# Retention projections of blocks 3 to 7: seven float32 products of matrix halves, or three float32r products of 12-bit parts

## The chip, the core and the metric

The kernel runs on one core of a Trainium2 chip. The metric is the device time of one launch in microseconds (us). The kernel before takes 971.28 us, the median of three runs (969.27 to 971.3).

## The reference, cut to what matters

The input x has 4 sequences of 1024 tokens with 512 channels. Two layers stand in a sandwich of layer norms.

```python
x = x + _layernorm(_L0_attn_ref(_layernorm(x)))    # retention
x = x + _layernorm(_L0_ffn_ref(_layernorm(x)))     # gated FFN, inner width 1536
# retention, on the normed x:
q = x @ Wq.T ; v = x @ Wv.T                        # 512 x 512 each
ret = _retention_scan(v, lam)                      # state = lam * state + v_t, per channel
out = _layernorm(q * ret)
out = (out * silu(x @ Wg.T)) @ Wo.T
# FFN: weights rounded to fp8 values
fuse = silu((x @ gate_w) * gate_scale) * ((x @ up_w) * up_scale)
y = (fuse @ down_w) * down_scale
```

So every block of tokens has four square projections (v, q, g and o, 512 by 512) and the three FFN products.

## The kernel before

**Blocks and loops.** The 4096 tokens are cut into 8 blocks of 512. The outer loop t runs over the FFN of block t (`Ffn`, gate, up, down). Beside it the same pass does the retention of block t+1 (`b`, class `Retention`) and prepares block t+2 (`n`: load, first norm, transposition through DRAM into `xnT`). The inner loop i runs over 12 slices of 128 inner channels. In a slice TensorE does `gate(i)`, `up(i)` and `down(i-2)`, 8 matmuls of 128x128 by 512 each, and between these groups the projections of the next block. One slice takes 5.4 to 12.4 us.

**FFN number format.** The fp8-valued weights are exact in float32r (F32R in the code, a 4-byte format that TensorE reads in fewer bits), and the activations are cut into an upper and a lower part, so `project` does two float32r matmuls for each 128 channels.

**Projections in blocks 2 to 7 (`b.fast`).** v, q, g and o are each done with seven products of matrix halves in place of eight (`order`, `banks`, `product`, `take`, `add_o`), in plain float32. A product is four float32 matmuls of 256 columns. It needs sums of halves of the input (`input_sums`, on GpSimd, kept in `t_sums`), sums of halves of the weights (formed in block 0's and block 1's passes and kept in DRAM by `keep_sums`), and additions of the results, on VectorE, into `mids`. The weights' halves come through a ring of four 256 KB buffers (`w_ring`, `fetch_weights`): after each product the DMA for the fourth product ahead is put on SyncE's queue, where it waits until its buffer is free.

**What sets the order.** `keep_in_program_order` makes each engine execute its instructions in the order in which the program names them, so the order is written out by hand with `if t == ... and i == ...`. PSUM has eight banks: two for the projections (`pa0`, `pa1`), two that gate and up of the FFN use in turn (`pf`), four for down. A matmul group that begins in a bank waits until the engine that read the bank's previous content is done. So `up(i+1)` waits until VectorE has done the fused multiplication `fuse(i)` (SCALAR_TENSOR_TENSOR gate<-pfu), and a product in `pa1` waits until VectorE or ScalarE has read the product before it there.

**The end of a pass.** In i = 9 to 11 VectorE does, in this order: moments of x1, `fuse(9)`, the norm of x1 for token groups 0 and 1 with their transposition, `o_moments(2)` and `(3)`, `rest(9)`, `fuse(10)`, moments of x1 for groups 2 and 3, their norms, `fuse(11)`, `rest(10)` and the lower parts of the next FFN's input (`rest_of`). The next pass's `gate(0)` needs all of these. At the same time GpSimd does four `input_sums` for block n, and n's first three products run in i = 11.

**Block 1's pass (t = 1).** At the end of i = 0 `output_sums` forms the sums of the halves of Wo in place in `wo_sb`, on VectorE, and `keep_sums` stores them. ScalarE checks the FFN weights for values over the fp8 range in the same pass (`find_over`).

The lines most spoken of later:

```python
        pg = ps_f.tile([P, TB], F32, tag="pf", name=f"pfg_{self.t}_{i}")     # gate
        self.pu = ps_f.tile([P, TB], F32, tag="pf", name=f"pfu_{self.t}_{i}")  # up
        dve.scalar_tensor_tensor(g, self.pu, us_sb[:, i : i + 1], g, ALU.mult, ALU.mult)  # fuse
        act.copy(f[:, 0, :], g)
        dve.tensor_tensor(f[:, 1, :], self.g.pop(i), f[:, 0, :], ALU.subtract)            # rest
```

## Time and profile before

| what | value |
|---|---|
| median of 3 runs | 971.28 us |
| profiled execution, first to last instruction (span) | 968.2 us |
| the rest of a run, by the median | 3.1 us |
| TensorE (PE) busy | 955.3 us, 99% |
| VectorE (DVE) busy | 677.9 us, 70% |
| ScalarE (ACT) busy | 406.1 us, 42% |
| GpSimd (POOL) busy | 283.2 us, 29% |
| mean granted TensorE clock | 0.997 |
| DMA | 119.04 MB, mean 123 GB/s |

For the profiled execution the profile has no time but its span; the 3.1 us are the difference to the median of the runs. Times within the profile are counted from the first instruction. Engines are called by the profile's short names. "a <- b" means that a is written from b; names are those of the program's tiles, with f32 and fp32r for the two formats. A TensorE busy share says little about its rate, since matmuls overlap; the distance between starts of groups does.

### The profile page before, as it was taken

To read this page: it belongs to the slowest core of one execution; us is meant where nothing else is said; L and a number is where in the kernel's file an instruction comes from. 1 tells how busy PE (TensorE), PEld (TensorE's weight loads), DVE (VectorE), ACT (ScalarE), POOL (GpSimd) and SP (SyncE) were. 2 spreads that over 40 slices of the span, in tenths; PEclk is the share of its full clock that TensorE was granted. 3 is DMA by queue.
4 is the path that set the end of the run, shared out by engine and by line. 5 is a ranking of instruction groups with operands and counts; after the bars stand their busy time and mean duration, and the time that the engine had idled before them with its cause. 6 is when DMAs were issued, how large, how long until landed. Compare 5 with 4: busy or idle time off the path is not lost.

```text
span 968.2 us, 11802 instructions
## 1 busy us (share of the span) xinstructions
PE 955.3 (99%) x4118; PEld 764.9 (79%) x4118; DVE 677.9 (70%) x1038; ACT 406.1 (42%) x637; POOL 283.2 (29%) x356
## 2 busy tenths in 40 slices
PE   9999999999999999999999999999999999999997
PEld 7455767778888888888888888888888888888885
DVE  5996999676768578575685766867667675747445
ACT  3555674468656135331433315332153421524223
POOL 1405121402327042250522415242142512314020
PEclk9999999999999999999999999999999999999998
DMA  9311423762436336463236523364242632314021
GB/s 297 128 53 57 152 66 96 221 217 86 142 97 180 126 91 214 127 191 95 97 109 175 161 80 126 103 171 146 77 152 87 184 121 77 109 44 131 0 88 44
DMA packets 96060, 119.04 MB, mean 123 GB/s; under 512 B 8320, under 2 KB 58240, under 8 KB 96000
## 3 DMA queue, kind: packets, MB, share of 16 engines
q1 hardware_dynamic: 95136, 117.62, 39.6%
q8 instruction: 33, 0.54, 0.2%
q10 hardware_dynamic: 864, 0.66, 0.2%
q14 instruction: 27, 0.22, 0.1%
HBM read 86.00 MB, written 32.24 MB: 122 GB/s over the span
## 4 chain that ended last, share of the span: by engine, by line
PE 87%; DVE 6%; DMA 2%; ACT 2%; POOL 1%; issue 1%; SPq 0%; DVEq 0%; ACTq 0%; POOLq 0%
PE pfg L74 16%; PE pfu L74 16%; PE pd L74 15%; PE pq L74 10%; PE pv L74 10%; PE pg L74 9%; PE po L74 8%; DVE scr L74 1%; DVE st L74 1%; DVE y L74 1%; PE pt L74 1%; DMA xnT<-mx 1%; ACT x1n L74 1%; DVE gate L74 1%; POOL mv L74 1%
## 5 line engine op out<-in xcount | busy, mean ns | idle before, releaser
L74 PE MATMUL pfu<-x1nT,up_sb 128*128 128x512 f32 x768 | 205.1, 409 | 0.0
L74 PE MATMUL pfg<-x1nT,gate_sb 128*128 128x512 f32 x768 | 198.1, 400 | 0.1
L74 PE MATMUL pd<-down_sb,fuse 128*128 128x512 f32 x720 | 189.4, 405 | 0.0
L74 PEld LDWEIGHTS pfu<-x1nT,up_sb 128*128 128x128 f32 x768 | 144.5, 188 | 32.1 <-issue 3.1
L74 PEld LDWEIGHTS pfg<-x1nT,gate_sb 128*128 128x128 f32 x768 | 144.2, 188 | 30.3 <-DVE x1nT L74 0.9
L74 PEld LDWEIGHTS pd<-down_sb,fuse 128*128 128x128 f32 x720 | 135.4, 188 | 27.3
L74 ACT ACTIVATE gate<-pfg,gs_sb 128x512 f32<-128x512 f32 x96 | 65.5, 682 | 169.1 <-PE pfg L74 168.9
L74 ACT CAST fuse<-gate 128x512 fp32r<-128x512 f32 x90 | 55.6, 618 | 176.3 <-DVE gate L74 176.2
L74 DVE SCALAR_TENSOR_TENSOR gate<-pfu,us_sb,gate 128x512 f32<-128x512 f32 x96 | 71.8, 748 | 57.9 <-PE pfu L74 56.5
L74 POOL TENSOR_SCALAR mv<-mv 128x1 f32<-128x1 f32 (+1 forms) x82 | 23.5, 286 | 264.0 <-DVE mv L74 260.8
L74 DVE TENSOR_TENSOR fuse<-gate,fuse 128x512 fp32r<-128x512 f32 x90 | 76.8, 853 | 5.5 <-ACT fuse L74 5.5
L74 POOL TENSOR_TENSOR ysum<-y 128x256 f32<-128x256 f32 (+1 forms) x14 | 14.3, 1024 | 195.7 <-DVE y L74 195.7
L74 DVE BATCH_NORM_STATS2 st<-x 128x6 f32<-128x512 f32 x64 | 43.6, 681 | 29.4 <-POOL x L74 26.2
L74 POOL TENSOR_TENSOR mv<-mv,nhalf 128x1 f32<-128x1 f32 (+1 forms) x75 | 48.6, 649 | 6.2
L74 PE MATMUL pv<-t_sums,w_ring 128*128 128x256 f32 x192 | 45.5, 380 | 0.5 <-POOL t_sums L74 0.5
L74 PE MATMUL pg<-t_sums,w_ring 128*128 128x256 f32 x192 | 45.7, 381 | 0.0
L74 PE MATMUL po<-w_ring,t_sums 128*128 128x256 f32 x192 | 45.4, 379 | 0.0
L74 POOL TENSOR_TENSOR x<-x,x1n 128x512 f32<-128x512 f32 x32 | 41.5, 1296 | 13.2 <-ACT x1n L74 12.8
L74 PE MATMUL pq<-t_sums,w_ring 128*128 128x256 f32 x192 | 45.3, 379 | 0.0
L74 PEld LDWEIGHTS pv<-t_sums,w_ring 128*128 128x128 f32 x192 | 36.1, 190 | 6.6 <-POOL t_sums L74 0.7
L74 PEld LDWEIGHTS pg<-t_sums,w_ring 128*128 128x128 f32 x192 | 35.9, 190 | 6.5 <-ACT mids L74 1.3
L74 PEld LDWEIGHTS po<-w_ring,t_sums 128*128 128x128 f32 x192 | 36.2, 189 | 6.0 <-issue 0.3
(168 smaller groups left out, 1512.5 us busy)
## 6 DMA issues: line engine op xcount, KB each, us to landing
kept<-x SPq DMA_DIRECT2D x32, 256.0 KB, 3.0
x<-kept SPq DMA_DIRECT2D x32, 256.0 KB, 4.1
x<-in_x SPq DMA_DIRECT2D x28, 256.0 KB, 4.3
out<-d SPq DMA_DIRECT2D x27, 256.0 KB, 2.0
xnT<-mx SPq DMA_DIRECT2D x24, 256.0 KB, 4.9
w_ring<-dsum_v SPq DMA_DIRECT2D x24, 256.0 KB, 3.5
w_ring<-dsum_q SPq DMA_DIRECT2D x24, 256.0 KB, 2.6
w_ring<-dsum_g SPq DMA_DIRECT2D x24, 256.0 KB, 2.6
```

Of the source, the lines that this page charges most:

```text
L74: return lambda *args, **kwargs: tc.keep_in_program_order(op(*args, **kwargs))
```

## The change

Block 2 keeps its seven products per projection. In blocks 3 to 7, v, q and g are done with three float32r products instead; o stays as it was. A number is cut into its upper 12 bits (`top`) and the rest (`low`); `diff` holds a scaled difference of the two. Each of the four 128-channel output slices c of a projection gets three passes of four matmuls of 512 columns: top times top, low times low, then ScalarE multiplies the bank in place by 1 + 2**-12, and diff times diff completes the sum (`begin`, `end`, placed by the table `gaps`). After that v's slice is scanned, q's multiplied and g's given to Silu directly from the bank.

The parts of x are formed for each of the five blocks in i = 9 and 10 of the pass before (`tops_of`, `lows_of`, `diffs_of`), in quarters of 128x512 elements. The parts of the weights are formed once, in block 1's pass, 12 units of 128x512 (`Splitter`), stored to DRAM and fetched through a second ring in 36 pieces per block where 21 halves were fetched.

```diff
     def output_sums():
-        operands["o"] = {1: v[:, 0:2, 0:H], 2: v[:, 2:4, 0:H], 3: v[:, 2:4, H:D]}
+        operands["o"] = {}
+        made["o"] = {1: b11, 2: b21, 3: b22}
+        keep_sums("o")
         made["o"] = {5: b11, 7: b12, 6: b22, 4: b21}
         dve.tensor_tensor(b11, b12, b11, ALU.subtract)
...
+    class Splitter:
+            self.room = wpool.tile([P, 4, D], F32, tag="wo_sb", name="split_room")
...
+        def load(self, n):
+                src = self.sources[k].rearrange("(c p) f -> p c f", p=P)[:, :, ts(c, P)]
+                sp.dma_start(w.rearrange("p (c f) -> p c f", c=NC), src)
...
+                sp.dma_start(parts["top"].rearrange("p (c f) -> p c f", c=NC), src)
...
+        def split(self):
+                dve.tensor_scalar(top.bitcast(I32), w.bitcast(I32), TOP_MASK, None, ALU.bitwise_and)
+                dve.tensor_tensor(w, w, top, ALU.subtract)
+                dve.scalar_tensor_tensor(top, top, -LOW, w, ALU.mult, ALU.add)
+                pool.tensor_scalar(w, w, 1.0 / LOW, 1.0, ALU.mult, ALU.mult)
...
+        def store(self):
+                self.load(self.n + 1)
+                sp.dma_start(operands[k, c]["diff"], top)
+                sp.dma_start(operands[k, c]["low"], w)
...
+    gaps = {
+        -2: [("begin", "v", 0)], -1: [("end", "v", 0), ("begin", "v", 1)],
+        0: [("end", "v", 1)], 1: [("begin", "v", 2)], 2: [("end", "v", 2), ("begin", "v", 3)],
...
+        13: [("begin", "g", 1)], 14: [("end", "g", 1)], 15: [("begin", "g", 2)],
+        16: [("end", "g", 2)], 17: [("begin", "g", 3)], 18: [("end", "g", 3)],
...
+    def tops_of(self, *which):
+                dve.tensor_scalar(top, x, TOP_MASK, None, ALU.bitwise_and)
+    def lows_of(self, *which, engine=dve):
+                engine.tensor_tensor(self.quarter(self.low, k), x, top, ALU.subtract)
+    def diffs_of(self, *which):
+                dve.scalar_tensor_tensor(
+                    self.quarter(self.diff, k), low, -1.0 / LOW, top, ALU.mult, ALU.add
+                )
...
+    def begin(self, k, c, home):
+            bank = self.bank[k, c] = ps_tile(f"p{k}{c}_{self.t}", home)
+            self.pass_of(bank, k, c, "top")
+            self.pass_of(bank, k, c, "low")
+            act.activation(bank, bank, AF.Copy, scale=1.0 + LOW)
...
     def var(self):
-            var = ps_tile(f"var_{self.t}", "pa1" if self.fast else "pa")
+            var = ps_tile(f"var_{self.t}", "pa0" if self.by_parts else "pa1" if self.fast else "pa")
...
+            if t == 1 and 1 <= i < 9:
+                splitter.split()
...
+            if fast and i == 10 and n:
+                n.diffs_of(0, 1)
...
+            if t == 1 and i in (2, 3, 4, 7):
+                splitter.store()
+                splitter.split()
...
                 if n:
-                    n.input_sums(1, 2)
+                    n.new_parts()
+                    n.tops_of(0, 1, 2, 3)
+                    n.lows_of(0, 1, engine=pool)
+                    n.lows_of(2, 3)
...
                 b.x1_moments(2)
                 b.x1_moments(3)
+                if n:
+                    n.diffs_of(2, 3)
...
+            if t == 1 and 1 <= i < 9:
+                splitter.store()
```

Where these stand in the order: the first `split` of a slice comes after `gate(i)` and the projection work that follows it; the second, in i = 2, 3, 4 and 7, after `up(i)` and before `fuse(i)`, directly behind the load of its unit; `store` ends a slice. `tops_of` and `lows_of` come in i = 9 after the norms of x1's groups 0 and 1, `diffs_of(0, 1)` in i = 10 before `up(10)` and `fuse(10)`, `diffs_of(2, 3)` after x1's moments of groups 2 and 3 and before their norms. `gap(3i)`, `gap(3i+1)` and `gap(3i+2)` follow `gate(i)`, `up(i)` and `down(i-2)`; gap -2 and -1 lie in i = 11 of the pass before.

## The prediction

> **What bounds the kernel now.** I read the page first, then the chain, then the timelines of PE and DVE at the end of a pass, last the stretch of block 1's pass that gets the weight split.

> The page and its chain of waits:

> ```profile
> PE 955.3 (99%) x4118; PEld 764.9 (79%) x4118; DVE 677.9 (70%) x1038; ACT 406.1 (42%) x637; POOL 283.2 (29%) x356
> ...
> PE 87%; DVE 6%; DMA 2%; ACT 2%; POOL 1%; issue 1%; SPq 0%; DVEq 0%; ACTq 0%; POOLq 0%
> ```

> PE is the bound nearly throughout, so fewer matmul columns count in full, and so does every new wait of PE.

> Groups of instructions (busy, mean ns): the two matmul kinds that change places.

> ```profile
> L74 PE MATMUL pd<-down_sb,fuse 128*128 128x512 f32 x720 | 189.4, 405 | 0.0
> L74 PE MATMUL pv<-t_sums,w_ring 128*128 128x256 f32 x192 | 45.5, 380 | 0.5 <-POOL t_sums L74 0.5
> ```

> Mean durations overlap and are no rate; the distance of starts is. The timeline of PE in i = 10 and 11 of the pass t = 3 (start, duration, both in us):

> ```profile
> 648.53 1.98 PE L74 MATMUL pfu<-x1nT,up_sb 128*128 128x512 f32 x8
> 650.34 1.98 PE L74 MATMUL pd<-down_sb,fuse 128*128 128x512 f32 x8
> 652.15 1.98 PE L74 MATMUL pfg<-x1nT,gate_sb 128*128 128x512 f32 x8
> 653.97 1.98 PE L74 MATMUL pfu<-x1nT,up_sb 128*128 128x512 f32 x8
> ```

> Eight float32r matmuls take 1.815 us from start to start, 0.227 each. The last line is `up(11)`. Now DVE at the same time:

> ```profile
> 645.57 0.75 DVE L74 SCALAR_TENSOR_TENSOR gate<-pfu,us_sb,gate 128x512 f32<-128x512 f32 x1
> 646.24 0.54 DVE L74 TENSOR_SCALAR x1n<-x,mv 128x512 f32<-128x512 f32 x1
> 646.81 0.71 DVE L74 STREAM_TRANSPOSE xs<-x1n 128x512 f32<-128x512 f32 x1
> 647.44 1.32 DVE L74 TENSOR_SCALAR x1n<-x,mv 128x512 f32<-128x512 f32 x1
> 648.80 0.71 DVE L74 STREAM_TRANSPOSE xs<-x1n 128x512 f32<-128x512 f32 x1
> ...
> 651.59 0.75 DVE L74 SCALAR_TENSOR_TENSOR gate<-pfu,us_sb,gate 128x512 f32<-128x512 f32 x1
> 653.79 0.70 DVE L74 BATCH_NORM_STATS2 st<-x 128x6 f32<-128x512 f32 x1 [1.46 <-POOL x L74]
> ```

> The two SCALAR_TENSOR_TENSOR are `fuse(9)` and `fuse(10)`. `up(11)` writes the bank that `fuse(10)` reads until 652.34: DVE is 1.6 us early there. From 643.27 to 664 DVE stands still for only 2.0 us in all, so this end of a pass has little room on DVE, whatever its 70% says. The second x1n shows how DVE fares beside POOL: 1.32 us for 0.54.

> Block 1's pass, i = 1, where DVE and ACT free a bank for PE; the timelines of DVE, ACT and PE:

> ```profile
> 217.03 0.75 DVE L74 SCALAR_TENSOR_TENSOR gate<-pfu,us_sb,gate 128x512 f32<-128x512 f32 x1
> ```

> ```profile
> 217.82 0.62 ACT L74 CAST fuse<-gate 128x512 fp32r<-128x512 f32 x1 [2.86 <-DVE gate L74]
> 218.34 0.58 ACT L74 COPY mids<-pq 128x512 f32<-128x512 f32 x1
> ```

> ```profile
> 219.65 1.89 PE L74 MATMUL pq<-xnT,w_ring 128*128 128x256 f32 x8
> ```

> The second q product (219.65) follows the copy of the first, out of the same bank, by 0.7 us; that copy stands on ACT behind the cast, which waits for DVE.

> **Matmuls: -18.0.** In the chain two products, 16 records, take 3.46 us: 1.73 each. Per block 21 x 1.73 = 36.3 go and 36 passes x 4 x 0.227 = 32.7 come: -3.6, times 5 blocks -18.0. Between float32 products eight float32r matmuls take 1.83 (0.229): by that -16.5. [...]

> **Off the path.** Per block DVE loses 15 additions into mids (0.69) and scans stay level (8 x 0.73 to 4 x 1.25), POOL loses four input sums (1.3 to 1.5), ACT gains 12 copies in place (0.59) and loses three: 5.3 us at 42% busy. From `begin` to `end` of a slice at least eight matmuls (1.8) lie between, and a copy takes 0.59 after its wait: hidden, at 0.6 to 1.2 to spare. If ACT were late, `end` would wait as long.

> **End of a pass: +22.5.** Here DVE gets, between its 648.8 and `fuse(10)`: four tops, two lows, two of the diffs; POOL two lows. On the clock of t = 3: x1n of group 1 no longer meets POOL's sums (0.54, not 1.32), so its transposition ends at 648.64. Tops: nearest row TENSOR_SCALAR 128x512, 0.54, 0.45 apart: 1.8. Lows: TENSOR_TENSOR 0.61 apart: 1.2. POOL's two lows, 1.28 each: the 1.32 row shows a DVE instruction held until POOL's (647.19 to 648.48) ends, and 657.44 to 660.6 shows the two engines in turn. So 2.56 more: 654.2. Then moments 1.58, `rest(9)` 0.58, two diffs 0.67 apart, `fuse(10)` 0.74: done at 658.45. `up(11)` would start at 653.97 and waits 4.5. What is late behind it: moments of x1 and norms of groups 2 and 3, 24.6 us after gate(9) where 19.6 was; these lie within the 4.5 by which PE is late, and the next `gate(0)` waits no longer. Bounds: without turns 1.9; tops at 0.61, 5.1. I take 4.5, since both rows of turns are of this same place. Passes t = 1 to 5 have it: 22.5 (9.5 to 25.5).

> [...]

> **Variance: +2.** ACT's table load (1.28, at 598.42) ran ahead of var; now Silu of g1 comes between, var lies in pa0, and `begin g2` needs that bank 1.8 us later. Silu 0.6 + load 1.28 + root 0.69 end 2.6 us after `end g1`, PE is there 2.4 after. The half of the squares' sum also had 0.9 to spare and PE comes 1.5 sooner. I take 0.4, from 0 to 0.9, times 5.

> **Weight split: +14.** First wait: three added stores of wo_sb precede the in-place sums (DVE 0.6 later), the four stores of sums land at 217.8 (2.5 after issue, the dsum_o row), and only then may SP load unit 0 into the same room. Landing: 2.5 (dsum_o) to 4.9 (xnT<-mx, also 512-byte runs); I take 3.7, so 221.6. DVE waits there in order; split 0.45 + 0.61 + 0.67 = 1.75; `fuse(1)` ends at 224, not 217.8; ACT cast and copy of q1 end at 225.3; the second q product starts near 225.5 for 219.65: 6. Behind DVE's wait stand all bank reads; behind SP's wait the ring's fetches, which lead by four products (10 us) and suffice. The other 11 splits: 19.3 us of DVE. Windows of i = 2 to 8 (69.0 us) have DVE busy 48.9, so 20.1 idle. They would just fit, but in i = 3 to 6 mean, var and the first o product hang on DVE, and the four splits that follow a load at once (i = 2, 3, 4, 7) wait for it. By that 0 to 14 more; I take 8, a little over the middle, since three chains of PE hang on it. Sum 14 (with the landing at 2.5 and no more waits 5, up to 20).

> **DMA: 0.** 15 more fetches of 256 KB per block at 0.38 us of SP each; ring fetches land in 2.6 to 3.5 us, and the shortest lead over four passes is 4.6 us. Uncovered, up to 1 per block.

> **Sum.** -18.0 + 22.5 + 2 + 14 = +20.5. The profiled span 968.2 becomes 988.7; with the 3.1 us that the median has over the span, 991.8.

> **Rivals.** *DVE has room (faster).* POOL's lows cost DVE no turns, tops go 0.35 apart, splits fall into its idle time: end of a pass 1.5, split 5: -18 + 7.5 + 0 + 5 = -5.5, 965.8; with both at zero 953.3. It decides where the wait of `up(11)` is under 2.4 us and the split under 6. For it: 30% of DVE is idle. Against: little of that lies in these places. Chance 0.22, of it 0.18 faster and 0.04 within the bound.

> *The ring starves (slower still).* i = 0 moves 1 MB of x<-kept beside six fetches, 2.5 MB in 11 us or 230 GB/s, near the 240 of the busiest window; 2 us per block more, and the split at its upper end: 991.8 + 10 + 6 = 1008. Chance 0.10.

> *The passes aren't single.* [...] The FFN's rows show one record per float32r matmul: chance 0.01.

> The forecast has 0.67, its own range 976 to 1003, of it 0.01 within the bound. 0.2% is about what a measurement of this kernel can tell from no change. Faster 0.18, same 0.05, slower 0.77. Range 962 to 1003: half of the faster rival and the slower one stay out.

> **What would show it.** In t = 1 to 5 PE waits 4 to 5 us before pfu of i = 11 for DVE gate; DVE is without idle time from x1n to `fuse(10)`, tops or lows beside POOL last over 1.2. In t = 1 pq waits about 6 us for ACT, mu and po for DVE. Passes of pv, pq, pg are 0.91 us apart. The prediction is wrong if `up(11)` follows `gate(11)` at once, or if passes need over 0.95.

## The result and the profile after

The changed kernel takes 1019.77 us, the median of four runs (1014.49 to 1025.17), the kernel before 970.83, of four as well: a ratio of 1.051 (95% interval 1.047 to 1.055). The forecast was 991.8 us with a range of 962 to 1003. The direction was right and the size was not: slower by 49 us where 20.5 were summed up. The profiled execution is the slowest of the four, 1025.17 us with a span of 1023.2; against the span before, 968.2, that is 55.0 us.

The page of the changed kernel: busy times, chain, granted clock in 40 slices, and the costliest group (busy us and mean ns, then PE's idle time before it).

```profile
PE 969.1 (95%) x3998; PEld 757.9 (74%) x3998; DVE 673.8 (66%) x1039; ACT 432.6 (42%) x682; POOL 283.2 (28%) x343
...
PEclk9999999999898899998999999998999999999999
...
PE 52%; DVE 9%; ACT 3%; DMA 2%; issue 2%; POOL 2%; SPq 1%; DVEq 0%; ACTq 0%; POOLq 0%
...
L74 PE MATMUL pfu<-x1nT,up_sb 128*128 128x512 f32 x768 | 208.4, 415 | 17.0 <-DVE gate L74 17.0
```

PE's share of the chain fell from 87 to 52%, and pfu, which had no idle time worth naming, now stands 17.0 us for DVE's gate (the fused multiplication). The clock row has dips, something the forecast had no term for. Before it was

```profile
PEclk9999999999999999999999999999999999999998
```

A table by passes says where the time went. The windows view, cut at the passes' first gate matmul (length, then busy us of each engine, granted clock), gives for t = 1, t = 3 and t = 6 of the changed kernel:

```profile
197.81:357.21 159.40, 134.06 (x523) 107.37 (x521) 109.41 (x178) 78.22 (x114) 46.00 (x57) 0.89 0.58 185
...
479.97:599.55 119.58, 115.97 (x502) 94.91 (x500) 75.67 (x119) 45.32 (x75) 36.02 (x42) 0.97 0.52 156
...
838.20:948.67 110.47, 110.25 (x489) 90.83 (x488) 62.12 (x96) 41.89 (x70) 30.05 (x36) 1.00 0.44 135
```

Before, these passes took 116.6, 116.5 and 113.2 us, with PE busy throughout at a clock of 1.00. The line of t = 1:

```profile
197.77:314.35 116.58, 116.50 (x527) 97.94 (x525) 84.15 (x132) 77.91 (x114) 38.09 (x47) 1.00 0.46 137
```

So t = 1 lost 42.8: 25.3 in which PE stood (159.40 - 134.06), and about 17 by the clock, which lay at 0.50 for 34 us of this pass. Passes t = 2 to 5 lost 2 to 6 each. Only t = 6, where no further block is prepared and no parts are formed, is shorter, by 2.7.

**The end of a pass.** PE around `up(11)` of t = 3 (start, duration, and in brackets the wait with what ended it):

```profile
582.29 1.97 PE L74 MATMUL pfg<-x1nT,gate_sb 128*128 128x512 f32 x8
587.64 3.78 PE L74 MATMUL pfu<-x1nT,up_sb 128*128 128x512 f32 x8 [3.38 <-DVE gate L74]
591.22 1.91 PE L74 MATMUL pv<-xnT,w_ring_parts 128*128 128x512 f32 x4
592.93 1.29 PE L74 MATMUL pv<-low,w_ring_parts 128*128 128x512 f32 x4
```

DVE at the same place:

```profile
578.75 3.59 DVE L74 TENSOR_SCALAR top<-xnT 128x512 int32<-128x512 int32 x4
582.25 1.28 DVE L74 TENSOR_TENSOR low<-xnT,top 128x512 fp32r<-128x512 f32 x2
...
585.64 1.28 DVE L74 SCALAR_TENSOR_TENSOR diff<-low,top 128x512 fp32r<-128x512 f32 x2
586.85 0.74 DVE L74 SCALAR_TENSOR_TENSOR gate<-pfu,us_sb,gate 128x512 f32<-128x512 f32 x1
```

The chain is the forecast's: four tops (3.5 us, GpSimd's two lows beside them), lows, diffs, `fuse(10)` done at 587.59, and `up(11)` at 587.64. But `up(11)` then runs at half rate. From its start to the next group's it takes 3.58 us, and the next two passes, 0.95 and 0.91 elsewhere, take 1.71 and 1.13. The windows around it (clock behind the busy times):

```profile
582.30:586.50 4.20, 1.96 (x9) 1.31 (x7) 4.13 (x10) 1.34 (x4) 1.81 (x4) 1.00 0.47 125
586.50:593.30 6.80, 5.66 (x13) 4.45 (x14) 5.84 (x12) 2.38 (x5) 5.03 (x7) 0.50 0.21 77
593.40:600.00 6.60, 6.60 (x34) 5.48 (x33) 4.31 (x8) 3.47 (x7) 0.00 (x0) 1.00 0.44 119
```

The clock fell to 0.50 while PE still waited and stayed there for 6.8 us, 5.7 of them behind the wait of 3.4 us; they cost another 2.8 us. It fell when PE had stood 2.3 us (584.26 to 586.5), and in t = 1 a wait of 1.82 us was enough, the first line below; the windows behind it have the clock before and after its fall:

```profile
294.90 2.74 PE L74 MATMUL po<-w_ring,y 128*128 128x256 f32 x8 [1.82 <-issue]
```

```profile
293.00:296.40 3.40, 1.58 (x7) 1.10 (x7) 3.33 (x6) 2.22 (x3) 0.00 (x0) 1.00 0.00 0
296.40:299.80 3.40, 3.40 (x10) 2.66 (x9) 1.72 (x3) 1.83 (x4) 0.00 (x0) 0.50 0.33 107
```

**Block 1's pass.** Waits in t = 1 (who for whom: total, times, longest):

```profile
DVE split_room L74 <- DMA split_room<-in_wgT: 6.5, 2, 3.5
...
DVE split_room L74 <- DMA split_room<-in_wvT: 6.0, 2, 3.3
...
DVE split_room L74 <- DMA split_room<-in_wqT: 3.7, 2, 2.4
PEld pq L74 <- ACT mids L74: 4.5, 1, 4.5
```

DVE stands 16.2 us for landings of the split's loads, in six waits, and PE behind DVE or ACT.

### The profile page after: what moved, and what is told of

Same layout as the page of the kernel before. It is cut to its first block, busy times and chain, and to the rows that moved or that the text cites. A ratio compares the mean times of both kernels' runs of the same rounds, so it can differ in the third digit from the quotient of the medians.

```text
span 1023.2 us, 11854 instructions
## 1 busy us (share of the span) xinstructions
PE 969.1 (95%) x3998; PEld 757.9 (74%) x3998; DVE 673.8 (66%) x1039; ACT 432.6 (42%) x682; POOL 283.2 (28%) x343
## 4 chain that ended last, share of the span: by engine, by line
PE 52%; DVE 9%; ACT 3%; DMA 2%; issue 2%; POOL 2%; SPq 1%; DVEq 0%; ACTq 0%; POOLq 0%
PE pfu L74 11%; PE pfg L74 10%; PE pd L74 10%; PE po L74 6%; PE pv L74 6%; PE pq L74 5%; PE pg L74 3%; DVE top L74 2%; DVE st L74 2%; DVE gate L74 1%; SPq L74 1%; POOL sqsum L74 1%; DMA w_ring_parts<-dlow_g 1%; DVE diff L74 1%; DVE low L74 1%
## 5 line engine op out<-in xcount | busy, mean ns | idle before, releaser
L74 PE MATMUL pfu<-x1nT,up_sb 128*128 128x512 f32 x768 | 208.4, 415 | 17.0 <-DVE gate L74 17.0
L74 PE MATMUL pfg<-x1nT,gate_sb 128*128 128x512 f32 x768 | 196.3, 398 | 0.1
L74 PEld LDWEIGHTS pfu<-x1nT,up_sb 128*128 128x128 f32 x768 | 150.2, 196 | 53.6 <-DVE gate L74 19.1
L74 PE MATMUL pd<-down_sb,fuse 128*128 128x512 f32 x720 | 182.2, 395 | 0.0
L74 PEld LDWEIGHTS pfg<-x1nT,gate_sb 128*128 128x128 f32 x768 | 146.0, 190 | 31.2 <-DVE x1nT L74 0.8
L74 PEld LDWEIGHTS pd<-down_sb,fuse 128*128 128x128 f32 x720 | 135.2, 188 | 27.9
L74 ACT CAST fuse<-gate 128x512 fp32r<-128x512 f32 x90 | 55.7, 619 | 202.4 <-DVE gate L74 202.4
L74 DVE SCALAR_TENSOR_TENSOR gate<-pfu,us_sb,gate 128x512 f32<-128x512 f32 x96 | 71.7, 747 | 57.1 <-PE pfu L74 53.4
L74 ACT ACTIVATE gate<-pfg,gs_sb 128x512 f32<-128x512 f32 x96 | 65.6, 684 | 83.9 <-PE pfg L74 83.8
L74 POOL TENSOR_SCALAR mv<-mv 128x1 f32<-128x1 f32 (+1 forms) x82 | 24.3, 297 | 250.6 <-DVE mv L74 247.6
L74 DVE TENSOR_TENSOR fuse<-gate,fuse 128x512 fp32r<-128x512 f32 x90 | 73.2, 814 | 5.5 <-ACT fuse L74 5.5
L74 POOL TENSOR_TENSOR ysum<-y 128x512 f32<-128x512 f32 (+1 forms) x9 | 11.5, 1280 | 193.6 <-DVE y L74 193.6
L74 DVE BATCH_NORM_STATS2 st<-x 128x6 f32<-128x512 f32 x64 | 43.6, 681 | 19.2 <-POOL x L74 16.6
L74 POOL TENSOR_TENSOR mv<-mv,nhalf 128x1 f32<-128x1 f32 (+1 forms) x75 | 53.8, 717 | 6.2
L74 DVE TENSOR_TENSOR y<-pq,y 128x512 f32<-128x512 f32 x21 | 14.5, 691 | 46.3 <-PE pq L74 46.3
L74 POOL TENSOR_TENSOR x<-x,x1n 128x512 f32<-128x512 f32 x32 | 41.7, 1312 | 11.1 <-ACT x1n L74 11.0
L74 POOL TENSOR_TENSOR d<-d,x 128x512 f32<-128x512 f32 x28 | 36.4, 1321 | 21.7 <-ACT d L74 19.8
L74 POOL TENSOR_TENSOR sqsum<-sqsum,sq 128x512 f32<-128x512 f32 x24 | 35.0, 1458 | 15.2 <-ACT sq L74 13.6
L74 PE MATMUL po<-w_ring_parts,t_sums 128*128 128x256 f32 x160 | 37.8, 379 | 0.4 <-issue 0.4
L74 DVE STREAM_TRANSPOSE xn<-xn 128x512 f32<-128x512 f32 x20 | 14.2, 708 | 34.3 <-ACT xn L74 34.3
L74 DVE RECIPROCAL rstd<-rstd 128x512 f32<-128x512 f32 x8 | 26.8, 3352 | 14.0 <-ACT rstd L74 14.0
L74 ACT ACTIVATE pv<-pv 128x512 f32<-128x512 f32 x20 | 11.6, 582 | 57.3 <-PE pv L74 57.3
```

The costliest lines, as they stand in the source:

```text
L74: return lambda *args, **kwargs: tc.keep_in_program_order(op(*args, **kwargs))
```

## The experiments

Theory: (a) DVE's added work at the end of a pass makes PE wait, and the wait makes the clock fall; (b) the split makes DVE stand for landings. Rivals: the ring's 36 fetches or the passes themselves are slow; the split's cost is DVE's arithmetic, or its transfers on SyncE's queue. All kernels, with ratio to the kernel before (95% interval) and lengths of the passes in the profiled execution, from gate(0) to gate(0):

| kernel | us | ratio | t=1 | 2 | 3 | 4 | 5 | 6 |
|---|---|---|---|---|---|---|---|---|
| before | 970.8 | 1 | 116.6 | 116.4 | 116.5 | 116.2 | 117.1 | 113.2 |
| after | 1019.8 | 1.051 | 159.4 | 122.8 | 119.6 | 119.5 | 119.2 | 110.5 |
| e1_fill | 1012.5 | 1.044 (1.042-1.046) | 158.7 | 119.4 | 117.0 | 117.0 | 117.0 | 110.4 |
| e2_order | 1022.2 | 1.054 (1.052-1.057) | 159.8 | 120.1 | 119.0 | 119.2 | 119.6 | 110.5 |
| e3_no_split | 996.2 | 1.027 (1.022-1.031) | 132.2 | 121.3 | 119.7 | 119.6 | 119.2 | 110.5 |
| e4_order_no_split | 998.0 | 1.028 (1.026-1.029) | 134.2 | 122.4 | 117.6 | 119.0 | 119.5 | 110.5 |
| e5_no_x_parts | 1000.7 | 1.031 (1.029-1.033) | 153.7 | 116.6 | 114.3 | 114.3 | 115.8 | 111.4 |
| e6_late_parts | 1004.7 | 1.035 (1.034-1.037) | 150.9 | 118.8 | 115.4 | 115.5 | 115.5 | 113.9 |
| e7_bare | 964.6 | 0.994 (0.992-0.995) | 118.8 | 116.6 | 114.3 | 114.3 | 115.2 | 111.4 |
| e8_no_loads | 1004.1 | 1.036 (1.032-1.040) | 141.9 | 121.3 | 119.6 | 119.6 | 117.4 | 110.5 |
| e9_spaced_split | 1009.1 | 1.040 (1.038-1.042) | 148.6 | 121.0 | 118.6 | 116.9 | 119.0 | 110.5 |
| e10_late_and_spaced | 994.9 | 1.025 (1.023-1.026) | 141.7 | 118.7 | 115.4 | 115.4 | 116.0 | 113.9 |
| e11_copies | 985.7 | 1.016 (1.012-1.020) | 123.2 | 119.8 | 118.5 | 117.0 | 118.6 | 110.5 |

**e1_fill: is it the clock?** PE's wait before `up(11)` is filled with matmuls whose result nobody reads.

```diff
+        if n and n.by_parts and i == 11:
+            fill = ps_tile(f"fill_{t}", "pa1")
+            for _ in range(14):
+                pe.matmul(fill, mean_r, gate_sb[:, 0, 0:D], start=True, stop=True)
         f.up(i)
```

> Fourteen useless float32r matmuls (3.2 us) stand before up(11) in the passes t = 1 to 5, where PE waits 3.5 us for fuse(10). Theory: the wait is DVE's, and what follows it runs slowly only because PE stood idle (granted clock 0.50 over up(11) and the first pass of v0). Then the wait for fuse(10) still ends at the same place, but up(11) takes 1.82 us from start to start in place of 3.58, the first v0 pass 0.91 in place of 1.71, a pass 116.7 in place of 119.5 us, and the whole 14 us less: near 1006. [...]

```profile
578.25 1.98 PE L74 MATMUL pfg<-x1nT,gate_sb 128*128 128x512 f32 x8
580.07 3.43 PE L74 MATMUL fill<-gate_sb,mean_r 128*128 128x512 f32 x14
583.62 2.11 PE L74 MATMUL pfu<-x1nT,up_sb 128*128 128x512 f32 x8
585.56 1.11 PE L74 MATMUL pv<-xnT,w_ring_parts 128*128 128x512 f32 x4
```

`up(11)` starts as long after gate(11) as without the fill (5.37 and 5.35 us), but takes 1.94 to the next group, not 3.58. The passes t = 3 to 5 are 2.2 to 2.6 us shorter: by useless work, so this much is the clock. In all the run wins 7 us where 14 were expected, since t = 1 hardly moved.

**e2_order and e4_order_no_split: is it `fuse(10)`?** Half of the parts' operations are put behind it, so that it can run early.

```diff
-                    n.lows_of(2, 3)          # i = 9, before fuse(10)
...
-            if fast and i == 10 and n:
-                n.diffs_of(0, 1)
...
             f.fuse(i)
+            if fast and i == 10 and n:
+                n.lows_of(2, 3)
+                n.diffs_of(0, 1)
```

> DVE's two lows and the first two diffs stand behind fuse(10) in place of before it; nothing is left out. Theory: fuse(10) ends 2.4 us earlier, up(11) waits 1.1 us in place of 3.5, the clock doesn't fall (2.8 us more), so each of five passes is 5.2 us shorter and the total 26 less: near 994. Rival: the same DVE work still has to end before the last norms of x1, so the wait moves to the turn of x1n or to gate(0); then only the clock's part or less is won: 1006 to 1020.

The timeline of PE in e2_order:

```profile
583.49 2.11 PE L74 MATMUL pfu<-x1nT,up_sb 128*128 128x512 f32 x8 [0.99 <-DVE gate L74]
...
591.50 0.63 PE L74 MATMUL pt<-ident,x1n 128*128 128x128 f32 x4 [2.24 <-DVE x1n L74]
592.52 1.11 PE L74 MATMUL pt<-ident,x1n 128*128 128x128 f32 x4 [0.40 <-DVE x1n L74]
```

The wait of `up(11)` shrinks to 1.0 and comes back at the transposition of x1n, with the low clock behind it (0.57 from 592 to 596, after waits of only 2.24 and 0.40). All of DVE's work up to x1n(3) stands in one row, and what is taken from its middle is met at its end. The rival was right, and not even its 1006 to 1020 were reached: nothing was won (1022.2).

e4 has this order and leaves out the split's arithmetic (as e3 below; the weights' parts are then other numbers).

> Both edits: lows and diffs behind fuse(10), and the split's arithmetic left out. Theory: both terms go (26 and 35 us), near 959: what is left of the change is 3.3 us of matmuls per block, less 1 us of waits: 12 under the 971 of before. Rival: the passes of a block aren't shorter by themselves, then it stays at 971 or above.

Measured 998.0, no better than e3's 996.2 without the new order: a clear miss, which agrees with e2.

**e5_no_x_parts: is it this work at all?** The three kinds of operations are left out.

```diff
-                    n.tops_of(0, 1, 2, 3)
-                    n.lows_of(0, 1, engine=pool)
-                    n.lows_of(2, 3)
...
-                n.diffs_of(0, 1)
-                    n.diffs_of(2, 3)
...
-            x = {"top": self.by_chunk, "low": self.low, "diff": self.diff}[part]
+            x = self.by_chunk
```

> The changed kernel without the parts of x: no tops, lows and diffs are formed, all three passes of a slice read xnT itself (so the projections of blocks 3 to 7 are other numbers); passes, ring, copies and the weight split stay. Theory (it is the whole DVE and GpSimd work on these parts, with the clock that falls behind it, that lengthens the end of a pass): all 6.4 us of each end vanish, the passes t = 2 to 5 come to 113.2 us, 3.3 under the kernel before, t = 1 to 153; 1019.8 - 5 x 6.4 = 988 us. Rival (the ring's 36 fetches, the copies in place, or the order of the passes cost it): the passes stay at 117 or over, 1006 us or more.

Passes t = 3 and 4 fall from 119.5 to 114.3, without any wait at their ends. They miss the 113.2 by 1.1. Most of that is a side effect of the edit: all passes now read xnT, and such a pass takes 0.95 us, one that reads low or diff 0.91 (24 passes x 0.04 = 0.96). The ring's 36 fetches and the order of the passes cost nothing that is seen in these passes, so the rival falls there. In all, 1000.7 lies between theory (988) and rival (1006): t = 2 and t = 5 (116.6, 115.8) won less than expected, and 4.8 of the difference are the reads of xnT.

**e6_late_parts: is there room later?** Two tops stay in i = 10, all else is formed behind the last x1nT; v's slices go in pairs. Nothing is left out.

```diff
-        -2: [("begin", "v", 0)], -1: [("end", "v", 0), ("begin", "v", 1)],
-        0: [("end", "v", 1)], ...
+        -2: [("first", "v", 0)], -1: [("first", "v", 1)],
+        0: [("second", "v", 0), ("second", "v", 1)], 1: [("end", "v", 0), ("end", "v", 1)], ...
...
                 b.rest_of(3)
+                if n.by_parts:
+                    n.tops_of(2, 3)
+                    n.lows_of(0, 1, engine=pool)
+                    n.lows_of(2, 3)
+                    n.diffs_of(0, 1, 2, 3)
```

> The changed kernel with the parts of x formed later: two tops in DVE's idle time before x1n(2), all else after the last x1nT; v's slices in pairs, so that only the top passes, which read xnT, lie before the pass ends, low passes behind gate(0), diff passes behind fuse(0). Nothing is left out. Theory (DVE's serial work up to x1n(3) sets the end of a pass, behind it there is room): passes t = 2 to 5 of 113 to 114.5 us, t = 1 153 to 155; 990 to 996 us. Rival (DVE has no room in the next slice 0 either: low passes wait for lows, up(1) for fuse(0) behind the diffs): passes of 118 or more, 1012 us or more.

Passes t = 3 to 5 are 4 us shorter than in the changed kernel, and `up(11)` waits no longer. What is left is a wait of gate(0) for the last x1nT, since fewer matmuls lie before it:

```profile
PE pfg L74 <- DVE x1nT L74: 1.3, 1, 1.3
```

So most of the cost was the place, not the work: 4 us of the 6.2 that e5 wins without its side effect. But three of block n's passes move into its own pass, and t = 6 (113.9) shows them; in all, 1004.7 missed the 990 to 996.

**e3_no_split, e8_no_loads, e9_spaced_split, e11_copies: what of the split costs?** e3 leaves out the arithmetic, e8 ten of twelve loads, e11 all but one copy per unit; e9 keeps everything and puts splits, stores and loads at equal distances.

```diff
         def split(self):                       # e3
-                dve.tensor_scalar(...); dve.tensor_tensor(...); ...
+                pass
...
-                sp.dma_start(w..., src)        # e8
+                if n < 2:
+                    sp.dma_start(w..., src)
...
-            if t == 1 and i in (2, 3, 4, 7):   # e9
-                splitter.store()
-                splitter.split()
+                splitter.point(3 * i)          # after gate(i); odd: split, even: store and next load
...
+                splitter.point(3 * i + 1)      # after fuse(i)
...
+                splitter.point(3 * i + 2)      # at the end of the slice
```

> The four operations of the weight split (three on DVE, one on POOL) are left out; its loads and stores stay, so the parts' weights are wrong numbers. Theory: DVE's wait for each load and its 1.75 us per unit make the 43 us by which block 1's pass grew, apart from 6.3 of the end of the pass; that pass falls from 159 to 124 us, the total by 35 to near 985. Rival: the 48 added DMAs on SP's queue keep the ring of weights late; then PE waits for w_ring, the pass stays above 145 and the total above 1005.

> The changed kernel, with only the first two of the split's twelve loads into its room; the arithmetic of all twelve splits, the copies of top and all stores stay (the parts of ten units are other numbers). Theory (DVE stands for landings, 16.2 us in 7 waits of up to 3.5 us, and PE behind DVE): t = 1 falls from 159.4 to about 140, total about 1000 us. Rival (DVE's 21.7 us of arithmetic fills the pass): t = 1 stays over 155, total over 1015 us. Without the arithmetic, but with the loads, it was 132.

> The changed kernel with the weight split placed otherwise, nothing left out: the twelve splits stand 1.5 gaps of a slice apart in i = 1 to 8 (after gate, after fuse, or at the end of a slice, in turn), each store and the next load half way between two splits, where four splits followed their load at once. Theory (DVE stands for landings, 17.5 us in t = 1 by the run without loads): most of it is covered, t = 1 falls from 159.4 to 143 to 148 us, 1004 to 1009 us in all. Rival (the arithmetic on DVE holds PE up wherever it stands): t = 1 stays at 155 or over, 1015 us or more.

> The changed kernel with its parts of x, but without the split: no loads, arithmetic and stores, one copy of each weight slice serves as all three parts (so the projections of blocks 3 to 7 are other numbers). Theory (costs in t = 1 add up: end of the pass 5.7, split with all its transfers 34.8): t = 1 of 124.6 us, other passes as in the changed kernel; 1019.8 - 34.8 = 985 us. Against the run with transfers but without arithmetic (996.2) this gives the transfers alone, 7.7 us by the sum. Rival (transfers cost nothing of their own; the 7.7 is the end of the pass): t = 1 over 130 us, 992 us or more.

t = 1 was 159.4. It falls by 17.5 without the loads, 27.2 without the arithmetic (then nothing on DVE waits for a load either), 36.2 with one copy per unit instead of everything, and 10.8 with everything in place but spaced. The 17.5 are about half of the 36.2, and the theory puts them down to standing for landings. But e8 also takes ten transfers off SyncE's queue, and where all of them stay and only the place changes (e9), 10.8 come back; no run separates the rest. Transfers alone (e3 against e11) cost 9 us, by about which e3 missed the 124 that were expected. How, ACT's timeline shows, first in e3_no_split, then in the kernel before:

```profile
290.11 0.81 ACT L74 ACTIVATE xn<-x,mv 128x512 f32<-128x512 f32 x1 [9.03 <-DMA mx<-xn]
```

```profile
280.88 0.81 ACT L74 ACTIVATE xn<-x,mv 128x512 f32<-128x512 f32 x1 [2.85 <-DMA mx<-xn]
```

SyncE's queue issues `mx<-xn` at 285.76, behind the split's loads and stores of 283.11 to 285.24, 3.9 us after its data are there (DVE's transposition ends at 281.83); ACT waits for its buffer, DVE's transposition for ACT, an addition from a po bank stands behind that on DVE, and po waits 5.2 us. In the changed kernel ACT's longest such wait is 2.9, probably since PE is late there by other causes: the parts of t = 1 do not simply add up, one cure uncovers the next wait. e9 has the same: DVE's waits for loads fall from 16.2 to 4.5 us, but PE now waits for `po` twice, 5.4 and 4.4 us. The first of these follows DVE's norm of y, which stood behind a split of 1.87 us (284.98 to 286.85).

e11 also has a natural control for the clock. Windows of two ends of a pass in one execution, from gate(11) on:

```profile
543.40:548.70 5.30, 1.98 (x9) 1.31 (x7) 5.23 (x11) 2.29 (x6) 2.89 (x5) 1.00 0.34 107
548.70:551.00 2.30, 2.24 (x7) 1.76 (x8) 1.43 (x4) 1.42 (x3) 2.13 (x4) 0.66 0.30 114
...
661.91:667.20 5.29, 1.98 (x9) 1.31 (x7) 5.22 (x11) 2.27 (x6) 2.87 (x5) 1.00 0.45 110
667.20:669.20 2.00, 1.92 (x8) 1.61 (x9) 1.12 (x4) 1.44 (x3) 1.92 (x3) 1.00 0.33 125
```

PE waits 3.39 us at both. Once the clock falls and the pass takes 118.5, once it doesn't and the pass takes 117.0.

**e7_bare: what do the passes win?** The edits of e5 and e11 together.

> The changed kernel without the parts of x and without the split: all three passes read xnT and the same copy of the weight slice, written once by one transfer per unit in block 1's pass (so the projections of blocks 3 to 7 are other numbers); 36 fetches per block through the ring stay. Theory (the passes themselves win 3.3 us per block, and nothing else costs): passes t = 2 to 5 of 113.2, t = 1 of 114; 970.8 - 5 x 3.3 = 954 us. Rival (the ring or the new order of the products costs its share too): over 960 us; if nothing is won by the passes, 971.

964.6 us, 0.6% under the kernel before, with a clock of 0.998, where 954 was expected. Steady passes win 2.2 us, 3.2 without the strided reads of xnT (24 x 0.04). t = 1 and t = 2 win nothing: 118.8 for 116.6, and 116.6 for 116.4. In t = 2 of the changed kernel PE has two waits that may belong to this: 1.3 us of pg for the fetch `w_ring_parts<-dlow_g`, and 1.0 us of pv for DVE (`total`).

**e10_late_and_spaced: both cures, nothing left out.** e6 and e9 together, with the first two tops moved ahead of x1's moments.

> Both cures together, nothing left out: the parts of x formed late, with the first two tops moved ahead into DVE's wait of 1.46 us, and the split spaced evenly. Theory (the costs are separate and add up): t = 1 of 138 us (150.9 - 13), passes t = 2 to 5 of 114.6 (115.4 - 0.8); 1004.7 - 13 - 4 = 988 us, still slower than the kernel before, since the arithmetic and the transfers of the split stay. Rival (the causes share waits, one cure uncovers the other): 998 us or more.

994.9 us: 25 better than the changed kernel, 7 worse than expected, and still 2.5% slower than the kernel before. The tops' new place gave nothing (115.4 as in e6), and of the spacing's gain 9.2 us arrived. No complete version that was run beats the kernel before; even without split and parts 6 us were to be had.

## Why the prediction was wrong, step by step

By spans, before to e7 to e5 to the changed kernel, the 55.0 us are -4.5 for the bare passes, +35.4 for the split (999.1 - 963.7), +24.1 for the parts of x. With the strided reads of e5 and e7 taken out (5 blocks x 0.96) they become about -9.3, +35.4 and +28.9. The forecast's terms were -16 (matmuls and variance), +14 and +22.5. The profiled execution is the changed kernel's slowest; by medians the steps are -6.3, +36.1 and +19.1, and by the other way round, over e11, +21.1 for the parts of x and +34.1 for the split. So the split is the larger miss by any of these.

- **Matmuls, -18.0.** The records are single and the rate was right where low and diff are read, 0.91 per pass. Passes that read xnT in its strided layout take 0.95: 21 x 1.73 - (12 x 0.95 + 24 x 0.91) = 3.1 per block, so -15.5. The rest to -9.3 lies in t = 1 and t = 2 (2.3 and about 2.4 us) and at the two ends of the run; the two waits above may be part of it, the rest is not assigned.
- **Variance, +2.** PE waits 1.1 us in five times, for the half of the squares' sum. For the bank, the first of the two reasons that were given, no wait is seen.
- **End of a pass, +22.5.** The mechanism held: DVE slower beside GpSimd (four tops 3.5 us beside its two lows, where 1.8 was put for the tops alone; in e2_order two lows 2.39 beside its additions, 1.28 in the changed kernel), `fuse(10)` late, `up(11)` waiting. The wait was 3.4 to 3.5, not 4.5, because tops beside GpSimd took 3.5 in all instead of 4.36, and two diffs 1.2 instead of 1.34. The step that failed is the missing term behind it: the clock, 2.8 us for such a wait (in t = 5 it stayed low for only 3.4 us and cost 1.7). That the medians' 19.1, or 23.9 without the strided reads, come near 22.5 is luck: a shorter wait and a term left out. The lines that the prediction takes for t = 3 are those of t = 4, which runs from 547.26 to 663.48; this changes nothing in the sum. The remark that later norms lie "within the 4.5" was right, and e2 showed its other side: with `fuse(10)` early they are what PE waits for.
- **Weight split, +14.** The first wait was right: the second q product started at 224.86 (forecast 225.5), a split takes 1.81 (1.75). The failed step is the other eleven, taken at 8 from a range of 0 to 14. PE's 25.3 us of standing in t = 1, less 4.1 for the first wait, 0.6 ahead of it that e7 has too, and 3.5 at the end of the pass, leave 17.1; of the 17 by the clock about 12 are theirs (1.7 follow the first wait, 2.8 the end of the pass). That is some 29 in place of 8. The sum compared DVE's idle time with the arithmetic and gave the landings a place in the idle time; but four splits stood directly behind their own load, three of them waited 2.4 to 3.5 us for it, and every bank read stood behind DVE's wait. For the clock it had no term here either.
- **DMA, 0.** Right for the ring: in t = 2 to 7 PE waits once for a fetch, 1.3 us. Not right for block 1's pass, where transfers on SyncE's queue delay `mx<-xn` (e3).
- **Rivals.** "DVE has room" needed a wait under 2.4 and a split under 6: neither. "The ring starves" fell with e5 and e7. Slower still than the range is what came: by the split's place in DVE's order, which the forecast had named and sized at 8, and by the clock, which neither the forecast nor a rival named.

## What to carry to other kernels

When a change makes a saturated PE wait, price the wait at its length plus what the halved clock adds afterwards. Here that was 2.8 us behind most waits of 3.4 us and 1.7 behind one of 1.82; add a range from none to all of it, since the same wait of 3.39 us came with and without it. An engine at 70% has room only where its work does not stand in the row that PE waits for: e6 moved the same operations by some 10 us and won 4 us per pass. A step that loads, works and stores through two buffers should have its load a good landing time ahead of its use in the order of the waiting engine, since everything queued behind it there waits too: in t = 1 DVE stood 16.2 us for six landings, and with splits, stores and loads at equal distances (e9) the pass was 10.8 us shorter.
